# Routing the first expert layer in four parts of four tiles, and clearing the rows behind each expert with one indirect transfer

## The chip, the cores and the metric

The kernel runs on one core of one Trainium2 chip. The metric is the device time of one execution in microseconds (us). The profile is one execution recorded by the hardware profiler; its engines are PE (matrix multiply; PEld is its weight load), DVE (vector), ACT (scalar, activation functions), POOL (GpSimd, which also issues the indirect transfers) and SP (here a queue of transfers and register loads). Everything is float32.

## The reference

2048 tokens (8 sequences of 256) of width 128 pass six sub-layers, each added to the residual `x`:

```python
x = x + 0.5 * ffn0(layernorm(x))     # mixture of 8 experts, 2 of them per token
x = x + attention(layernorm(x))      # 16 heads of width 8
x = x + 0.5 * ffn0(layernorm(x))     # the same mixture and weights again
x = x + 0.5 * channel_mix(layernorm(x))
x = x + gated_conv(layernorm(x))
x = x + 0.5 * channel_mix(layernorm(x))
```

The change lies in the mixture, mostly in its first use:

```python
h = rmsnorm(x @ W_in.T, in_norm_w)
logits = h @ Wr.T
_, idx = top_k(logits + expert_bias, 2)
gates = softmax(logits[idx])         # zero for the experts that are not chosen
for e in range(8):
    oe = rmsnorm((silu(h @ Wg[e].T) * (h @ Wu[e].T)) @ Wd[e].T, enorm_w[e])
    out = out + gates[:, e:e+1] * oe
return rmsnorm(out, out_norm_w) @ W_out.T
```

## The kernel before

**Tiles and parts.** The tokens are 16 tiles of 128. `dispatch(f, i, parts, mp)` routes one part of the tiles for use `f` (0 or 1) of the mixture: `EARLY` lists the parts of the first use as (first tile, number of tiles), here (0, 2), (2, 2), (4, 4), (8, 4), (12, 4); `LATE` lists those of the second. A part is a list of nine or more stages: `turned` transposes x on PE and copies it out on ACT; `product` (two halves of up to two tiles) multiplies by the folded input weight, copies the result `u` and sums its squares on ACT; `measured` takes the layer norm's variance on DVE; `normed`, `logits` and `scaled` apply the norm; two `choice` stages find the two largest logits; `places` works out each token's row; `rows` scatters the tokens.

**Places.** Each expert owns a region of `REGION` = 2304 rows of the DRAM tensor `hss[f]`, and a token chosen by it takes the next free row. `prank` is that rank: a matmul with a triangle (earlier tokens of the tile, L418), one matmul with ones for each tile but the last of the part (earlier tiles of the part, L420), and one with `macc`, the counts of the earlier parts (L427). DVE then makes `at_row` (L437), the row numbers `pos`, and their integers `posi` (L445).

**Scatter.** `rows` issues two indirect transfers for each tile from POOL (L452), 128 rows of 516 bytes each: 32 for the whole use.

**Order.** `stagger(chunks, 4)` starts a part four stages after the one before it, so that two or three parts are interleaved. PE, DVE, ACT and SP run in the order in which the program issues, by hand; on POOL, what is marked with `keep_in_program_order` stays in order as well.

**Table, zeros, experts.** After the last part, `table` counts the rows of each expert (`pcnt`, L474) and works out on DVE which expert each of up to 24 row blocks belongs to and where it starts (`tab`; cast to integers by L528 and L531). For f = 0 it first calls `zeros(first)`, which writes 256 rows of zeros behind each expert's last row with eight transfers, four from SP and four from ACT; each one loads its row number into a register (L550) and writes 132 KB (L553). Then `experts` works through the blocks in the order `TURNS`: SP loads the expert number into a register and fetches the weights `w_f` (L593, 852 KB), loads the row number and fetches the rows `hst_f` (L599); PE turns them (`pht_f`, L605), DVE copies them (`ht_f`), PE multiplies by the gate and up weights (`pg_f`, `pu_f`, L615) and by the down weights (`py_f`, L638), and POOL scatters the results. A row fetch waits for all scatters and zeros of `hss[0]`. In the second use the zeros are written ahead of time by `clear_rows`, and rows are fetched ahead of weights.

**After it.** `attention` runs a written-out schedule of half steps in which the parts of the second dispatch are placed (`leaving`): the `places` of its three four-tile parts run inside the attention, the last two parts, of two tiles each, behind it.

Of the kernel before, what the change touches and what calls it, by code (L numbers as in the profile page):

```python
# [16 lines left out]
P = 128  # L17
# [30 lines left out]
EARLY = (0, 2), (2, 2), (4, 4), (8, 4), (12, 4)  # L48
# [16 lines left out]
def macaron_kernel(ctx: ExitStack, tc: tile.TileContext, a: dict, out: bass.AP):  # L65
# [44 lines left out]
    def pack(name, widths, rows=P):  # L110
# [10 lines left out]
    win, wr_t, inw, eb, tri, slot, base, order, tokid = pack(  # L121
        "pack1", [D, E, 1, E, P, 2, E, E, NCH * TPC * 2]
    )
    tokid = tokid.rearrange("p (t k) -> p t k", k=2).bitcast(I32)
# [4 lines left out]
    zero = const.tile([P, 2 * ROW], F32, tag="zero", name="zero")  # L129
    nc.vector.memset(zero, 0.0)  # L130
# [163 lines left out]
    nc.vector.tensor_reduce(wmean, win, AX.X, ALU.add)  # L294
    nc.vector.tensor_scalar(wmean, wmean, 1.0 / D, None, ALU.mult)
    nc.vector.tensor_scalar(win, win, wmean, None, ALU.subtract)
    wrn = const.tile([P, E], F32, tag="wrn", name="wrn")
    nc.vector.tensor_scalar(wrn, wr_t, inw, None, ALU.mult)
    pwr = bank("pwr", "sa")[:, 0 : D + E]
    nc.tensor.transpose(pwr[:, 0:D], win, ident)  # L300
    nc.tensor.matmul(pwr[:, D : D + E], win, wrn, start=True, stop=True)
    nc.scalar.copy(win_r, pwr)
# [17 lines left out]
    macc = const.tile([P, len(EARLY) + 1, E], F32, tag="macc", name="macc")  # L320
    nc.vector.memset(macc[:, 0, :], 0.0)

    def dispatch(f, i, parts, mp):
# [29 lines left out]
        def product(i):  # L353
# [9 lines left out]
            nc.scalar.copy(u, pp)  # L363
            sq = norm.tile([P, 2, D], F32, tag="sq", name=f"sqin_{n}_{i}")
            for j in range(2):
                t = 2 * i + j
                nc.scalar.activation(
                    sq[:, j], u[:, j, 0:D], AF.Square, accum_out=st["ss"][:, t : t + 1]
                )
# [43 lines left out]
        def places():  # L413
# [5 lines left out]
            for t in range(nt - 1):  # L419
                nc.tensor.matmul(  # L420
                    pr[:, t + 1 :, :],
                    ones,
                    mask[:, t : t + 1, :].to_broadcast([P, nt - 1 - t, E]),
                    start=False,
                    stop=False,
                )
            nc.tensor.matmul(  # L427
                pr, ones, macc[:, i : i + 1, :].to_broadcast(sh), start=False, stop=True
            )
            cnt = small.tile([P, E], F32, tag="cnt", name=f"cnt_{n}")  # L430
            nc.vector.tensor_reduce(cnt, mask.rearrange("p t e -> p e t"), AX.X, ALU.add)
            nc.vector.tensor_add(macc[:, i + 1, :], macc[:, i, :], cnt)
# [30 lines left out]
        if f == 0:  # L463
            return turned, *halves, measured, both(normed, logits, scaled), *choices, places, rows
        return turned, *halves, measured, normed, logits, scaled, *choices, places, rows

    def table(f, parts, mp):
# [5 lines left out]
        pc = bank(f"pcnt_{f}", "sb")[:, 0:E]  # L473
        nc.tensor.matmul(pc, ones, macc[:, len(parts), :], start=True, stop=True)  # L474
        cnt = t_([P, E], "cnt")
        nc.vector.tensor_copy(cnt, pc)
        if f == 0:
            first = t_([P, E], "first", I32)
            nc.vector.tensor_tensor(first, pc, base, ALU.add)
            zeros(first)  # L480
# [64 lines left out]

    def zeros(first):

        for e in range(E):
            queue = (nc.sync, nc.scalar)[e % 2]
            row = nc.values_load(  # L550
                first[0:1, e : e + 1], engines=[queue.engine], min_val=1, max_val=HS_ROWS - TT
            )
            ins = queue.dma_start(  # L553
                hss[0][bass.ds(row, TT), :].rearrange("(p r) w -> p (r w)", p=P), zero
            )
            tc.declare_no_dep(ins.ins, group="hs0", reason="rows of their own")
            tc.add_to_no_dep_group("hs0", ins.ins)
# [1026 lines left out]
```

## Time and profile before

| what | us |
|---|---|
| median of three runs (623.07 to 624.63) | 624.25 |
| the profiled execution's own time | 626.05 |
| its span, from the first to the last instruction | 624.1 |
| PE busy | 522.8 |
| DVE busy | 356.1 |
| ACT busy | 271.0 |
| POOL busy | 192.1 |
| first scatter of the first use starts on POOL | 16.67 |
| its last scatter starts | 63.57 |
| PE starts on the first expert block | 74.11 |

Positions in time are read from the start of the span. In a timeline line the first number is the start, the second how long the group took, then engine, line of the kernel, operation and tiles (written <- read); brackets hold the idle time of the engine before it and what ended it. "SPq" is the SP queue issuing a transfer. A waits line gives who waited for whom: total us, times, longest. The span is shorter than the execution's own time by what lies before the first and after the last instruction.

### The profile page before, as it was taken

How to read it: one execution, taken by the hardware profiler on the slowest of the kernel's cores; microseconds unless marked ns; L12 is line 12 of the kernel's file. 1: busy time of each engine (PE TensorE's matmuls, PEld its weight loads, DVE VectorE, ACT ScalarE, POOL GpSimd, SP SyncE). 2: the span in 40 equal slices, each digit the busy share in tenths (PEclk: the TensorE clock that was granted, in tenths of full speed). 3: DMA queues.
4: the chain of work that ended last, by engine and by line, in shares of the span. 5: the costliest groups of instructions: out<-in, count | busy, mean ns of one | idle time of the engine just before them, and what ended most of it. 6: DMA issues, size and time to landing. Idle time of an engine off the chain costs nothing.

```text
span 624.1 us, 11214 instructions
## 1 busy us (share of the span) xinstructions
PE 522.8 (84%) x3879; PEld 399.4 (64%) x3879; DVE 356.1 (57%) x1108; ACT 271.0 (43%) x662; POOL 192.1 (31%) x199
## 2 busy tenths in 40 slices
PE   4531299999989999899899987669999999889996
PEld 3521188898965555556556644449999984558884
DVE  3665255554443566767876884734444442777675
ACT  3532032222332455666765564213233232876265
POOL 0567135743343121001100446402333335520110
PEclk9999999999999999999999996599999998979999
DMA  6112647767723036408111001065778745000002
GB/s 224 35 38 94 202 154 211 207 194 219 218 79 102 27 43 174 168 35 257 51 49 22 26 26 51 31 217 178 216 222 252 216 137 147 1 0 2 2 1 67
DMA packets 38122, 71.70 MB, mean 115 GB/s; under 512 B 4587, under 2 KB 27922, under 8 KB 36912
## 3 DMA queue, kind: packets, MB, share of 16 engines
q1 hardware_dynamic: 33136, 61.97, 33.3%
q0 software_dynamic: 4352, 8.47, 3.9%
q8 instruction: 32, 0.52, 0.3%
q10 hardware_dynamic: 576, 0.53, 0.2%
q14 instruction: 26, 0.21, 0.1%
HBM read 50.10 MB, written 21.38 MB: 115 GB/s over the span
## 4 chain that ended last, share of the span: by engine, by line
PE 45%; ACT 9%; DVE 7%; DMA 5%; issue 3%; SPq 1%; POOL 0%; DVEq 0%; ACTq 0%; POOLq 0%
PE ps L967 8%; PE py_f L638 4%; PE pg_f L615 4%; PE pu_f L615 4%; ACT es L1004 4%; PE po L1014 4%; DMA y<-yrow_f,idx_f 3%; PE pvf L1343 2%; PE pgo L1370 2%; PE pm L950 1%; PE pk_m L1287 1%; DVE m L987 1%; PE pkv_m L1269 1%; PE pr_m L1269 1%; DMA w_f<-in_wall_dram 1%
## 5 line engine op out<-in xcount | busy, mean ns | idle before, releaser
L658 POOL DMA_INDIRECT y<-yrow_f,idx_f x72 | 70.7, 982 | 121.2 <-issue 61.8
L1004 ACT ACTIVATE es<-ps 128x1024 f32<-128x1024 f32 x64 | 65.3, 1020 | 51.7 <-PE ps L967 29.9
L987 DVE TENSOR_REDUCE m<-pm 128x4 f32<-128x1024 f32 x64 | 77.5, 1220 | 13.2 <-PE pm L950 13.1
L967 PE MATMUL ps<-qa,qk 32*128 32x256 f32 x512 | 72.8, 401 | 12.5 <-ACT es L1004 9.6
L452 POOL DMA_INDIRECT hs<-hrow,posi_f x64 | 61.7, 964 | 64.1 <-issue 28.7
L615 PE MATMUL pg_f<-ht_f,w_f 128*128 128x256 f32 (+1 forms) x336 | 71.5, 357 | 3.4 <-DMA w_f<-in_wall_dram 2.8
L638 PE MATMUL py_f<-w_f,hg_f 128*128 128x128 f32 x576 | 71.7, 276 | 2.4 <-issue 2.4
L950 PE MATMUL pm<-qk 32*128 32x256 f32 x512 | 73.1, 400 | 0.6 <-ACT qk L897 0.6
L638 PEld LDWEIGHTS py_f<-w_f,hg_f 128*128 128x128 f32 x576 | 69.5, 192 | 4.3 <-issue 2.7
L631 DVE TENSOR_TENSOR hg_f<-pu_f,sg_f 128x1024 f32<-128x1024 f32 (+1 forms) x42 | 45.0, 1071 | 43.4 <-PE pu_f L615 36.8
L615 PE MATMUL pu_f<-ht_f,w_f 128*128 128x256 f32 (+1 forms) x336 | 69.7, 350 | 0.0
L624 ACT ACTIVATE sg_f<-pg_f 128x1024 f32<-128x1024 f32 (+1 forms) x42 | 37.9, 901 | 59.5 <-PE pg_f L615 58.9
L967 PEld LDWEIGHTS ps<-qa,qk 32*128 32x128 f32 x512 | 43.6, 184 | 30.3 <-ACT es L1004 22.5
L648 ACT ACTIVATE ysq_f<-py_f 128x128 f32<-128x128 f32 x72 | 19.3, 273 | 99.6 <-PE py_f L638 92.1
L615 PEld LDWEIGHTS pg_f<-ht_f,w_f 128*128 128x128 f32 x336 | 56.1, 194 | 9.6 <-DVE hg_f L631 1.9
L615 PEld LDWEIGHTS pu_f<-ht_f,w_f 128*128 128x128 f32 x336 | 55.2, 192 | 5.6
L950 PEld LDWEIGHTS pm<-qk 32*128 32x128 f32 x512 | 44.2, 184 | 2.5 <-issue 1.5
L649 DVE TENSOR_TENSOR yrow_f<-py_f,w_f 128x256 f32<-128x256 f32 (+1 forms) x42 | 16.2, 387 | 45.0 <-ACT ysq_f L648 44.9
L607 DVE TENSOR_SCALAR ht_f<-pht_f,pack 128x256 f32<-128x256 f32 (+1 forms) x42 | 18.6, 444 | 33.5 <-PE pht_f L605 33.5
L605 PE MATMUL pht_f<-ident,hst_f 128*128 128x128 f32 x72 | 15.4, 283 | 24.5 <-DMA hst_f<-hs 24.5
L1014 PE MATMUL po<-es,v 128*32 128x256 f32 x512 | 35.7, 393 | 0.0
L161 POOL TENSOR_TENSOR cf_f<-cf_f,mhalf 128x8 f32<-128x8 f32 (+1 forms) x9 | 13.5, 1502 | 62.9 <-DVE cf_f L721 62.0
(271 smaller groups left out, 867.7 us busy)
## 6 DMA issues: line engine op xcount, KB each, us to landing
w_f<-in_wall_dram SPq DMA_DIRECT2D x41, 832.0 KB
hs<-blank SPq DMA_DIRECT2D x8, 1032.0 KB
hst_f<-hs SPq DMA_DIRECT2D x30, 129.0 KB
y_f<-y SPq DMA_DIRECT2D x14, 258.0 KB
pack<-in_pack_dram SPq DMA_DIRECT2D x1, 1729.0 KB
heads<-qkc SPq DMA_DIRECT2D x3, 512.0 KB
qk<-heads SPq DMA_DIRECT2D x12, 128.0 KB
y<-yrow_f,idx_f POOLq DMA_INDIRECT x72
```

Source lines behind the costliest of these rows:

```text
L452: ins = nc.gpsimd.indirect_dma_start(out=hss[f], out_offset=bass.IndirectOffsetOnAxis(ap=st["posi"][:, t, k : k + 1], axis=0), in_=hrow[:, ...
L615: nc.tensor.matmul(ph[:, k, :], w[t][:, o + k * P : o + k * P + P], ht[t], start=True, stop=True)
L624: nc.scalar.activation(sg, pg, AF.Silu)
L631: nc.vector.tensor_mul(hg[t], pu, sg)
L638: nc.tensor.matmul(py[:, s, :], hg[t][:, k, ts(s, P)], w[t][:, 2 * DFF + k * D : 2 * DFF + k * D + D], start=(k == 0), stop=(k == NFC - 1),)
L648: nc.scalar.activation(sq[:, s], py[:, s], AF.Square, accum_out=yrow[:, s, D : D + 1])
L658: ins = nc.gpsimd.indirect_dma_start(out=y2, out_offset=bass.IndirectOffsetOnAxis(ap=idx[:, s : s + 1], axis=0), in_=yrow[:, s, :], in_off ...
L950: nc.tensor.matmul(sc[:, jj, i, :], qs[c][r, g, col + i * P : col + (i + 1) * P], ks[c][r, g, col : col + S], start=True, stop=True,)
L967: nc.tensor.matmul(sc[:, jj, i, :], ks[c][r, g, col + i * P : col + (i + 1) * P], tops[s][r, :], start=True, stop=True,)
L987: nc.vector.tensor_reduce(m, sc, AX.X, ALU.max, negate=True)
L1004: nc.scalar.activation(es, sc, AF.Exp, scale=scale)
L1014: nc.tensor.matmul(po[32 * j : 32 * j + 32, :], vs[c][:, (b % 2) * 2 + i, (g % 2) * (H // 2) + (g // 2) * 4 + j, :], ess[s, j // 2][:, j % ...
```

## The change

- The first use is routed in four parts of four tiles, in place of five of which the first two had two tiles.
- In both uses the matmul for each tile of a part is dropped. DVE keeps a running count `ahead`, one entry for each tile, and one matmul with ones takes in the entries of the whole part.
- The first part's `u` is copied by DVE, while ACT squares straight out of PSUM; its `turned` and `measured` are issued in one stage.
- The input weight is folded inside a function `fold_in`, called after the attention's tiles are allocated; ahead of its matmuls PE multiplies the identity by itself nine times. DVE's norm statistics of the first part now come behind the folding.
- The eight zero transfers and their register loads are replaced by one indirect transfer from POOL: each of 128 partitions writes 16 rows (8256 bytes in a row) at a word offset that three small DVE operations work out. It stands behind the first scatter of the last part, with seven scatters behind it. Its source is part of an attention tile, set to zero by DVE at the start.
- `pcnt` is made ahead of the last part's `rows`.

```diff
-EARLY = (0, 2), (2, 2), (4, 4), (8, 4), (12, 4)
+EARLY = (0, 4), (4, 4), (8, 4), (12, 4)
...
-zero = const.tile([P, 2 * ROW], F32, tag="zero", name="zero")
-nc.vector.memset(zero, 0.0)
...
+    def fold_in():
...
+        warm_i = bank("warm_i", "sb")
+        for i in range(9):
+            nc.tensor.matmul(warm_i[:, ts(i % 4, P)], ident, ident, start=True, stop=True)
+        pwr = bank("pwr", "sa")[:, 0 : D + E]
+        nc.tensor.transpose(pwr[:, 0:D], win, ident)
+        nc.tensor.matmul(pwr[:, D : D + E], win, wrn, start=True, stop=True)
+        nc.scalar.copy(win_r, pwr)
...
-            nc.scalar.copy(u, pp)
+            first = f == 0 and t0 == 0
+            if first:
+                nc.vector.tensor_copy(u, pp)
+            else:
+                nc.scalar.copy(u, pp)
...
+                src = pp if first else u
                 nc.scalar.activation(
-                    sq[:, j], u[:, j, 0:D], AF.Square, accum_out=st["ss"][:, t : t + 1]
+                    sq[:, j], src[:, j, 0:D], AF.Square, accum_out=st["ss"][:, t : t + 1]
                 )
...
             nc.tensor.matmul(pr, tri, mask, start=True, stop=False)
-            for t in range(nt - 1):
-                nc.tensor.matmul(
-                    pr[:, t + 1 :, :],
-                    ones,
-                    mask[:, t : t + 1, :].to_broadcast([P, nt - 1 - t, E]),
-                    start=False,
-                    stop=False,
-                )
-            nc.tensor.matmul(
-                pr, ones, macc[:, i : i + 1, :].to_broadcast(sh), start=False, stop=True
-            )
-            cnt = small.tile([P, E], F32, tag="cnt", name=f"cnt_{n}")
-            nc.vector.tensor_reduce(cnt, mask.rearrange("p t e -> p e t"), AX.X, ALU.add)
-            nc.vector.tensor_add(macc[:, i + 1, :], macc[:, i, :], cnt)
+            for t in range(nt):
+                nc.vector.tensor_add(ahead[:, t0 + t + 1, :], ahead[:, t0 + t, :], mask[:, t, :])
+            nc.tensor.matmul(pr, ones, ahead[:, slots, :], start=False, stop=True)
...
+            start = both(normed, logits, scaled)
+            if i == 0:
+                return both(turned, measured), *halves, lambda: None, start, *choices, places, rows
+            return turned, *halves, measured, start, *choices, places, rows
...
+    def counts(f):
+        pc = bank(f"pcnt_{f}", "sb")[:, 0:E]
+        nc.tensor.matmul(pc, ones, ahead[:, NCH * TPC, :], start=True, stop=True)
+        return pc
+
+    def zeros(pc, mp):
+        at = mp.tile([P, E], F32, tag="zat", name="zat", bufs=1)
+        nc.vector.tensor_mul(at, pc, owner)
+        row = mp.tile([P, 1], F32, tag="zsum", name="zsum", bufs=1)
+        nc.vector.tensor_reduce(row, at, AX.X, ALU.add)
+        word = mp.tile([P, 1], I32, tag="zword", name="zword", bufs=1)
+        nc.vector.scalar_tensor_tensor(word, row, float(ROW), zrow, ALU.mult, ALU.add)
+        ins = nc.gpsimd.indirect_dma_start(
+            out=hss[0].rearrange("n w -> (n w)").unsqueeze(1),
+            out_offset=bass.IndirectOffsetOnAxis(ap=word, axis=0),
+            in_=blank[0],
+            in_offset=None,
+        )
...
-    def zeros(first):
-        for e in range(E):
-            queue = (nc.sync, nc.scalar)[e % 2]
-            row = nc.values_load(
-                first[0:1, e : e + 1], engines=[queue.engine], min_val=1, max_val=HS_ROWS - TT
-            )
-            ins = queue.dma_start(
-                hss[0][bass.ds(row, TT), :].rearrange("(p r) w -> p (r w)", p=P), zero
-            )
...
     def heads(hp):
         qks = [hp.tile([P, 2, 4, CT], F32, tag=f"qk{i}", name=f"qk{i}") for i in range(2)]
...
+        blank.append(qks[0].rearrange("p i g s -> p (i g s)")[:, 0 : 16 * ROW])
+        nc.vector.memset(blank[0], 0.0)
...
-            stagger([dispatch(0, i, EARLY, gp) for i in range(len(EARLY))], 4)
...
+                fold_in()
+                parts = [[*dispatch(0, i, EARLY, gp)] for i in range(len(EARLY))]
+                found = {}
+
+                def counted():
+                    found["pc"] = counts(0)
+                    zeros(found["pc"], gp)
+
+                parts[-1][-1] = both(counted, parts[-1][-1])
+                stagger(parts, 4)
...
+        "owner": p // 16 == e[None, :],
+        "zrow": ROW * (REGION * (p // 16) + 1 + 16 * (p % 16)),
```

## The prediction

> **What bounds the kernel now.** I read the page first, then who waited for whom in the first 80 us, then the timeline of that stretch, engine by engine.
>
> ```profile
> span 624.1 us, 11214 instructions
> ...
> PE   4531299999989999899899987669999999889996
> ...
> POOL 0567135743343121001100446402333335520110
> ```
>
> One slice is 15.6 us. From the sixth slice on PE is at 9 tenths nearly everywhere; ahead of that lie some 74 us in which PE does little. All the edits of weight lie there, so the question is what ends that stretch.
>
> ```profile
> PE pht_f L605 <- DMA hst_f<-hs: 21.8, 1, 21.8
> ```
>
> PE's longest wait by far is for the rows of the first expert block. Those need every scatter landed, the zeros landed, and SP free to issue the fetch. The timeline tells which was last:
>
> ```profile
> 16.67 1.17 POOL L452 DMA_INDIRECT hs<-hrow,posi_f  x1 [15.30 <-DVE z_f L351]
> ...
> 44.56 0.95 POOL L452 DMA_INDIRECT hs<-hrow,posi_f  x1 [1.77 <-issue]
> 45.82 0.95 POOL L452 DMA_INDIRECT hs<-hrow,posi_f  x1 [0.30 <-issue]
> ...
> 63.57 0.96 POOL L452 DMA_INDIRECT hs<-hrow,posi_f  x1 [0.30 <-issue]
> ```
> ```profile
> 55.09 12.76 SPq L553 DMA_DIRECT2D hs<-zero  x4
> 68.64 0.36 SPq L593 DMA_DIRECT2D w_f<-in_wall_dram  x1
> 69.86 0.41 SPq L599 DMA_DIRECT2D hst_f<-hs  x1
> ```
> ```profile
> 64.29 0.38 DVE L523 TENSOR_REDUCE tab_single<-tab_room 128x27 f32<-128x216 f32 x1 [3.12 <-issue]
> 66.39 0.18 DVE L528 CAST tab_tab<-tab_has 128x24 int32<-128x24 f32 x1 [0.50 <-DVE tab_has L524]
> 74.11 0.69 PE L605 MATMUL pht_f<-ident,hst_f 128*128 128x128 f32 x2 [21.82 <-DMA hst_f<-hs]
> ```
>
> Three chains end close together. POOL issues 32 scatters, one each 1.263 us (45.82 - 44.56) when it is fed; three times it isn't (gaps of 2.05, 4.58 and 1.77 us), and its last begins at 63.57. SP is held by four zero transfers until 67.85. DVE's table, begun at 52.4, has its first integers at 66.57: the same work without idle time is some 6 us, the rest is gaps of "issue". Then SP puts a weight load of 852 KB ahead of the row fetch, and the rows arrive 4.25 us after their issue (69.86 to 74.11). What this costs without SP's zeros is shown by the second use of the mixture, where the zeros are long written and rows are fetched ahead of weights:
>
> ```profile
> 404.83 0.96 POOL L452 DMA_INDIRECT hs<-hrow,posi_f  x1 [0.30 <-issue]
> 407.80 0.40 SPq L599 DMA_DIRECT2D hst_f<-hs  x1
> 410.17 0.42 PE L605 MATMUL pht_f<-ident,hst_f 128*128 128x128 f32 x2 [0.81 <-DMA hst_f<-hs]
> ```
>
> From the start of the last scatter to the fetch 2.97 us, to PE 5.34 us. Before the change the same distance is 10.54 us (63.57 to 74.11): 5.2 us are lost behind the scatters to SP and DVE, and 3 gaps of 8.4 us in all are lost ahead of them.
>
> **The change, part by part.**
>
> *When is the first part ready?* With two tiles its first scatter starts at 16.67. Four tiles add two transposes (0.21 each, by L337: four take 1.09, two 0.69) 0.4; a copy of 512 instead of 256 columns 0.2 (0.56 against 0.37); in product and squares 0.6 (two more matmuls take 0.9 and two more squares 0.6, but DVE now makes the copy of 0.39 beside ACT, and squares of half one run beside product two); eight or nine DVE steps on 32 instead of 16 columns 0.3. Then the rank's matmuls stand on PE behind the next part's product, which now has four matmul pairs (2.18 instead of 1.27), while one pair and 0.4 go: 0.5 to 0.8. Sum +2.0 to +2.3: 18.7 to 19.0. Against it stand the nine matmuls at the start. They need only the identity (ready at 1.37), are 18 passes at 0.21, 3.8 us, and end at 5.2, just where DVE has the folded weight ready (5.11), so they cost at most 0.3. Their worth is PE's clock:
>
> ```profile
> 75.43 3.75 PE L615 MATMUL pg_f<-ht_f,w_f 128*128 128x256 f32 x8 [0.62 <-issue]
> ...
> 81.38 1.89 PE L615 MATMUL pg_f<-ht_f,w_f 128*128 128x256 f32 x8
> ```
>
> The same eight matmuls take 3.75 us at the start and 1.89 after some 4 us of work. The Trainium skill ("TensorE: Matmul & The Clock Gate", Part 1) says the same of about 3.4 us of sustained work, and that one idle window of that length takes it back. By the first half the first part's transposes and products run at double pace (-1.3); by the second half PE's idle stretches of 3 to 4 us in the routing (4.16 ahead of the product at 27.12) make everything after that slow again. Trace alone (no warm start shown here): 18.9. Rule at its best, warm through part two: 16.7. I take warm for the first part only: 17.7.
>
> *Is POOL fed from then on?* A round of a four-tile part was 9.3 us (the `posi` of 22.7 to 32.06), of which DVE waited 2.41 for PE's rank:
>
> ```profile
> 27.12 2.18 PE L359 MATMUL pin_f<-win_r,xnt_f 128*128 128x136 f32 x8 [4.16 <-ACT xnt_f L339]
> ...
> 31.32 0.19 DVE L437 TENSOR_TENSOR at_row_f<-prank_f,pack 128x32 f32<-128x32 f32 x1 [2.41 <-PE prank_f L427]
> ```
>
> Three matmul pairs go (L420: 1.28); DVE loses a reduce and an add (0.38) and gains four adds in a row (0.2 each, from the 0.17 of macc's add and the step to the next), of which PE's second matmul needs three: 0.4 more DVE time, inside what is left of its wait. The round becomes 8.4. POOL needs 8 x 1.263 = 10.1 for a part, so it falls behind from the first part on and is never hungry; DVE gets 1.7 us of slack for each part. A stall such as the 4.66 us gap of DVE at 38 to 42.9 is covered from the second part on, and would cost up to 2 in the first.
>
> *POOL's chain.* 32 scatters and one zero transfer: the last starts 32 x 1.263 = 40.4 after the first, at 58.1. By the second use's distances the fetch follows at 61.1 and PE at 63.5: 10.6 earlier than 74.11.
>
> *The zeros.* No transfer of 8256 bytes from each partition is in the trace. On POOL's time: it has 128 rows and 128 offsets as a scatter has, so by the nearest row 0.96; if POOL paid for bytes, 16 rows' worth, 15.4. I take 0.96. On the DMA engines: 1.06 MB, issued at about 49; before the last scatter lands there are 7 x 1.263 + 2.5 = 11.3 us, 94 GB/s; the weights at 72 to 80 us ran at 357. Hidden. Its three DVE operations (0.5) are in slack. The rule against it: the skill's "SBUF — State Buffer" ("SBUF: two separate sides", the box on SWDGE and the part behind it) says that POOL can't write descriptors while DVE holds the port they share, and advises to issue from SP or ACT, the reverse of this edit. The trace disagrees for these shapes: at 44 to 64 DVE ran the choices and the table with two SBUF inputs, and POOL's pitch stayed 1.26 to 1.33. By the row the transfer costs 1.26; by the rule's 3.1 us for a blocked transfer, 2 us more.
>
> *Table and weights.* SP's zeros (12.8 us) and ACT's go whole. Part four's places end near 41; the table takes 14.2 us with the stalls of before, so SP can issue the first weights by 57 at the latest, without them by 49. They took 5.1 us to land (68.64 to 73.7), and the gate matmul needs them at 63.5 + 1.3. Covered by 2.9 us even with the stalls; beyond that each us of DVE is one of PE. The second weights are issued behind the first row fetch, as before, and PE needs them 7 us after its start, as before.
>
> *Second use.* For the three four-tile parts inside the attention PE waits for three adds behind DVE's `qa` (ended 339.47), where before the rank was done at 340.05: +0.35 each. In the last two parts one pair less, -0.43 each. Sum +0.2.
>
> *Other edits.* DVE's memset of 2064 columns (0.27 for 258; some 1.7 to 2.2) ends by 3.4, ahead of the pack, which DVE takes up at 4.27. The expert stage is unchanged and PE-bound, so the shift passes through.
>
> Sum: -10.6 + 0.2 = -10.4 on a span of 624.1, whose execution took 626.05, 1.8 over the median. I subtract from the median: 624.25 - 10.4 = 613.8.
>
> **Rivals.** *A. Part of it is taken back:* the first part comes late or POOL is hungry, the zero transfer costs 3 to 4, or the table's stalls grow past their cover of 2.9: 3 to 6 us lost, 617 to 620. For: DVE's gaps have no cause that the trace names. Against: POOL's queue grows by 1.7 a part.
> *B. Zeros priced by bytes on POOL:* the chain is then 14.4 longer, PE starts at 77.9, 3.8 later than before: 628. It decides from 11.6 us for that one instruction. Against: offsets, not bytes, are what it handles in every scatter seen.
> *C. The 74 us are not the bound:* if the expert stage had slack that took the shift, 624. Against: PE at 9 tenths, and `pg_f` L615 waits 3.4 us in 336 instructions.
>
> **Numbers.** Main forecast 0.75, A 0.15, B 0.05, C 0.03, and 0.02 for a gain under 0.3%. What a measurement of this kernel tells from no change is 0.3%, 1.9 us. The main range is 611 to 616 (first scatter at 16.7 to 18.9, second use -0.9 to +1); reaching into A gives 611 to 618. Faster 0.90 (main and A), same 0.05 (C and the small gain), slower 0.05 (B).
>
> **What would show it.** Right: the first scatter at 16.7 to 19; 33 POOL issues at a pitch of 1.26 without a gap over 0.5; the last near 58; the row fetch 3 us later with the first weights long issued; PE's first block near 63.5; the rest shifted by that. Wrong: a zero issue far over 1 us, gaps between POOL's parts, a weight load that lands after the rows, or an expert stage that grew.

## The result, and the profile after

The changed kernel takes 622.8 us (median of 22 runs, 618.9 to 630.3) where the kernel before takes 624.7 beside it: ratio 0.9962, interval 0.9944 to 0.998. The profiled execution took 623.28, its span is 621.5 against 624.1 before. So 2 to 3 us were gained where 10.4 were forecast, and the time lies above the range.

The page of the changed kernel, first by the slices of 15.6 us (busy tenths; PEclk is the clock that PE's throttle granted, in tenths of full speed):

```profile
span 621.5 us, 11085 instructions
...
PE   6411599999979999899899884669999998889996
...
POOL 0557146653333111101101345402343344520110
PEclk9655599999989999999999997599999998989999
```

PE's thin stretch still reaches into the fifth slice, and POOL has a slice with 1 tenth (the fifth: 62 to 78 us) behind one with 7: it was not through earlier. The timeline of the first 70 us shows the three chains that the prediction followed (start, duration, engine, line, tiles; in brackets the idle time before and who ended it):

```profile
6.44 1.12 PE L343 MATMUL pxt_f<-ident,x 128*128 128x128 f32 x4 [0.36 <-ACT win_r L306]
8.23 2.18 PE L365 MATMUL pin_f<-win_r,xnt_f 128*128 128x136 f32 x8 [0.68 <-ACT xnt_f L345]
19.23 1.17 POOL L453 DMA_INDIRECT hs<-hrow,posi_f  x1 [17.85 <-DVE amv_f L355]
...
38.38 0.95 POOL L453 DMA_INDIRECT hs<-hrow,posi_f  x1 [0.30 <-issue]
43.89 0.96 POOL L453 DMA_INDIRECT hs<-hrow,posi_f  x1 [4.55 <-issue]
...
55.25 0.96 POOL L485 DMA_INDIRECT hs<-qk,zword  x1 [0.30 <-issue]
...
64.30 0.96 POOL L453 DMA_INDIRECT hs<-hrow,posi_f  x1 [0.31 <-issue]
66.65 0.72 SPq L608 DMA_DIRECT2D hst_f<-hs  x1
68.81 0.69 PE L614 MATMUL pht_f<-ident,hst_f 128*128 128x128 f32 x2 [18.35 <-DMA hst_f<-hs]
```

POOL starts at 19.23, runs two parts without a gap, then waits 4.55 us for part two's places (counting from zero), and its last scatter begins at 64.30, later than before (63.57). The zero transfer costs POOL 0.96 us. The fetch follows the last scatter by 2.35 us, PE by 4.51: SP and the table are no longer in the way, and that is the whole gain at PE's first block, 74.11 to 68.81.

What did POOL wait for? DVE, ACT and PE in the same stretch:

```profile
29.48 0.19 DVE L417 TENSOR_REDUCE mx_f<-eq_f 128x4 f32<-128x32 f32 x1
...
32.84 0.19 DVE L415 TENSOR_TENSOR eq_f<-lb_f,mx_f 128x32 f32<-128x32 f32 x1 [1.23 <-DVE mx_f L413]
33.57 0.19 DVE L416 TENSOR_TENSOR eq_f<-eq_f,pack 128x32 f32<-128x32 f32 x1 [0.53 <-DVE eq_f L415]
34.27 0.19 DVE L417 TENSOR_REDUCE mx_f<-eq_f 128x4 f32<-128x32 f32 x1 [0.51 <-issue]
...
38.53 0.17 DVE L432 TENSOR_TENSOR ahead<-ahead,mask_f 128x8 f32<-128x8 f32 x1 [1.21 <-DVE ahead L432]
...
39.95 0.39 ACT L374 COPY u_f<-pin_f 128x272 f32<-128x272 f32 x1 [6.96 <-remote]
40.67 0.63 PE L433 MATMUL prank_f<-ahead,ones 128*128 128x32 f32 x2 [2.83 <-issue]
```

From 29.9 to 42.1 nearly each instruction starts 0.70 us, or twice that, after the one before it, on DVE, and ACT and PE stand as well, with nothing named that they wait for (`issue`, `remote`, their own last result). The instructions themselves take their usual 0.19. POOL alone goes on at its pitch as long as it has work. I call this a slow stretch. Code being loaded does not fill it: the profile counts one packet of instructions on the DMA queues from 28 to 44. Part two's places are done at 43.1 where a round of 8.4 us would have had them near 35. A second one lies on the table (55.5 to 65), hidden here by POOL. With this pattern known, the first trace has it too, at 56 to 67, where SP took 12.76 us for four zero issues, and in DVE's gap ahead of 42.88:

```profile
42.88 0.19 DVE L437 TENSOR_TENSOR at_row_f<-prank_f,pack 128x32 f32<-128x32 f32 x1 [4.66 <-remote]
```

PE's granted clock is low in the same slices of the changed kernel, but it is not the cause. From 20 to 72 us it is 0.51 here and 1.00 in the kernel before, which has slow stretches all the same, and one of the later profiles of the changed kernel (e14) has 0.52 from 12 to 68 and none.

### The profile page after: what moved, and what is told of

The parts are those of the page before. It is cut to its first block, busy times and chain, and to the rows that moved or that the text cites. A ratio compares the mean times of both kernels' runs of the same rounds, so it can differ in the third digit from the quotient of the medians.

```text
span 621.5 us, 11085 instructions
## 1 busy us (share of the span) xinstructions
PE 516.6 (83%) x3849; PEld 395.3 (64%) x3849; DVE 357.2 (57%) x1100; ACT 269.7 (43%) x658; POOL 193.2 (31%) x200
## 4 chain that ended last, share of the span: by engine, by line
PE 44%; ACT 10%; DVE 7%; DMA 5%; issue 2%; another core or an unknown queue 1%; SPq 1%; POOL 0%; DVEq 0%; ACTq 0%; POOLq 0%
PE ps L978 9%; PE py_f L647 4%; PE pg_f L624 4%; PE pu_f L624 4%; ACT es L1015 4%; PE po L1025 3%; DMA y<-yrow_f,idx_f 3%; PE pvf L1354 2%; PE pgo L1381 2%; DVE m L998 2%; PE pm L961 1%; PE pk_m L1298 1%; PE pr_m L1280 1%; PE pkv_m L1280 1%
## 5 line engine op out<-in xcount | busy, mean ns | idle before, releaser
L978 PEld LDWEIGHTS ps<-qa,qk 32*128 32x128 f32 x512 | 43.7, 184 | 30.3 <-ACT es L1015 21.8
```

The lines of the kernel that those rows point to most:

```text
L978: nc.tensor.matmul(sc[:, jj, i, :], ks[c][r, g, col + i * P : col + (i + 1) * P], tops[s][r, :], start=True, stop=True,)
```

## The experiments

Three chips did these runs: chip A (e1 to e4, e9 to e11; the kernel before takes 623.5 to 624.4 there), chip B (e5 to e8; 615.8) and chip C (e12 to e18; 615.5, and 620.9 in the last session). Ratios are to the kernel before on the same chip in the same session. Traces differ as much between chips as between kernels, so each reading below names its chip. Theory 1: a long train of scatters on POOL (one behind the other without a gap) slows the other engines. Theory 2: the stall belongs to a place in the instruction stream. Theory 3: only the late first part costs. The first pair of traces looks like chip A's. Theory 4 came after e5 to e8: the chip's condition decides whether there is a slow stretch at all.

**e1, every scatter of the first use twice** (chip A)

```
-                for k in range(2):
+                for k, to in ((0, hss[f]), (1, hss[f]), (0, spare), (1, spare))[: 2 if f else 4]:
...
-                        out=hss[f],
+                        out=to,
```

> Every scatter of the first use is issued a second time, into a DRAM tensor of its own that nobody reads; all else is the changed kernel. Theory 1 (an unbroken train of indirect transfers on POOL makes DVE, ACT, PE and SP step at about 0.70 us an instruction, from some 8 to 12 us after the train's first transfer until some 3 us after its last): a part now has 16 transfers, 20.2 us, more than a slow round, so the train is unbroken from 19.2 to about 99, and the slow stretch lasts from about 29 to about 102; DVE's steps in parts two, three and four and in the table are all 0.7 apart; PE's first block is at 106 or later. Theory 2 (the stall belongs to a place in the instruction stream[...]): DVE is slow in part two's places (29.9 to 42.1) and again in the table, and at full pace in part three, as in the changed kernel. Theory 3 (only the late first part costs; the slow stretches are chance): no stretch of 0.70 us steps need be there, parts come at 8.4 us.

POOL ran 48 transfers from 17.63 without a gap:

```profile
77.17 0.96 POOL L454 DMA_INDIRECT spare<-hrow,posi_f  x1 [0.30 <-issue]
86.18 0.95 POOL L486 DMA_INDIRECT hs<-qk,zword  x1 [8.05 <-DVE tab_cnt L503]
```
```profile
57.02 0.19 DVE L398 TENSOR_TENSOR lg_f<-u_f,ri_f 128x32 f32<-128x32 f32 x1 [2.38 <-remote]
58.42 0.19 DVE L410 TENSOR_TENSOR lb_f<-lg_f,pack 128x32 f32<-128x32 f32 x1 [1.21 <-DVE lg_f L398]
...
85.03 0.22 DVE L442 TENSOR_REDUCE pos_f<-both_f 128x8 f32<-128x64 f32 x1 [0.48 <-DVE both_f L440]
85.28 0.17 DVE L447 CAST posi_f<-pos_f 128x8 int32<-128x8 f32 x1
```

DVE's slow steps began near 29 and lasted to 85: the whole of part three, which ran at full pace in the changed kernel, now crept. When the train ran dry they stopped, some 8 us after its last transfer began (3 were expected). Theory 2 falls. Theory 1's detail was off in one point: slow parts took longer than the 20 us that POOL needs for one, so the train did break once, at 78. PE's first block came at 108.8, and the one execution took 667.2. The profile counts one packet of instructions from 28 to 86.

**e2, a memset of 192 columns on POOL behind every scatter of the first use** (chip A, one profile)

```
+                    if f == 0:
+                        tc.keep_in_program_order(nc.gpsimd.memset(pause, 0.0))
```

> A small memset on POOL after every scatter of the first use, so that the pitch becomes some 1.5 to 1.8 instead of 1.263 us. Theory 1, if it is the rate that fills something up: no slow stretch, parts two to four ready at the 8.4 us round (posi at about 18.9, 27.3, 35.7, 44.1), table without steps of 0.70; the last scatter 32 pitches after 19.2, at 67 to 77, and PE's first block 5.3 after it. Theory 1, if it is the unbroken train and not its rate: the slow stretch comes as in the changed kernel. Theory 2: slow at part two's places (29.9 to 42.1) all the same.

```profile
20.95 0.96 POOL L455 DMA_INDIRECT hs<-hrow,posi_f  x1 [0.17 <-issue]
21.91 0.27 POOL L465 MEMSET pause<- 128x192 f32 x1
22.35 0.97 POOL L455 DMA_INDIRECT hs<-hrow,posi_f  x1 [0.17 <-issue]
...
34.50 0.33 DVE L448 CAST posi_f<-pos_f 128x8 int32<-128x8 f32 x1
...
64.23 0.96 POOL L455 DMA_INDIRECT hs<-hrow,posi_f  x1 [0.17 <-issue]
68.71 0.69 PE L618 MATMUL pht_f<-ident,hst_f 128*128 128x128 f32 x2 [26.38 <-DMA hst_f<-hs]
```

At a pitch of 1.40 us POOL is never hungry, the parts' places come each 7.7 to 8.2 us (26.27, 34.50, 42.22), and apart from three steps at 43 to 45.4 the slow stretch is gone. It gained nothing: the pauses cost 32 x 0.137 = 4.4 us of POOL, as much as the hunger had, and PE starts at 68.71.

**e3, the old counting in the second use** and **e4, no warming matmuls** (chip A)

```
+            if f == 0:
...
+            else:
+                for t in range(nt - 1):
+                    nc.tensor.matmul(
+                        pr[:, t + 1 :, :],
...
+                    pr, ones, macc[:, i : i + 1, :].to_broadcast(sh), start=False, stop=True
...
+                nc.vector.tensor_reduce(cnt, mask.rearrange("p t e -> p e t"), AX.X, ALU.add)
+                nc.vector.tensor_add(macc[:, i + 1, :], macc[:, i, :], cnt)
```

```
-        warm_i = bank("warm_i", "sb")
-        for i in range(9):
-            nc.tensor.matmul(warm_i[:, ts(i % 4, P)], ident, ident, start=True, stop=True)
```

> The second use of the mixture counts as in the kernel before (matmul pairs and a running sum by part), the first use as in the changed kernel. Theory 1: the earlier rank joined two groups of scatters into one train of eight at 372 to 382; with the old rank the gaps of 0.85 and 0.95 us come back, the slow stretch is the 3 us of before instead of 8, and the 3.3 us that were lost between 375 and 420 return: profile span about 618, ratio to the kernel before about 0.991 (the changed kernel has 0.996). Rival (what is lost at 375 to 420 comes from the shift itself, not from the counts): span 621.5, ratio 0.996.

> The nine warming matmuls on the identity are left out; nothing of the result depends on them. If they do nothing for PE's clock in the first part (as the changed kernel's 2.18 us for eight product matmuls at 8.23 suggests): pwr at about 5.1, first scatter at 18.9 to 19.3, ratio to the kernel before 0.996 as with them. If they warm it for part of the way: first scatter 0.3 to 1.3 later, PE's first block and the end later by the same, ratio 0.997 to 0.998.

e3 gave 0.9889 (0.9833 to 0.9945, six runs), its profile a span of 619.2. That is near the number of theory 1, but its trace does not bear the reason: one gap of 2.48 us did come back into the train, and yet DVE stood still between 373 and 381 again,

```profile
376.57 0.16 DVE L387 SCALAR_TENSOR_TENSOR ri_f<-ss_f,z_f 128x2 f32<-128x2 f32 x1 [3.45 <-ACT u_f L376]
380.75 0.17 DVE L392 RECIPROCAL ri_f<-ri_f 128x2 f32<-128x2 f32 x1 [4.03 <-ACT warm L133]
```

and the way from the attention's last maximum to the second experts' first product took 51.3 us, against 49.7 in the changed kernel. Most of this standing still is PE and not a slow stretch. PE's granted clock is 0.50 from 368 to 380, and the four product matmuls there take 1.28 us, where the changed kernel's first profile has 1.00 and 0.73. The changed kernel on chip C (e18), with 0.50 from 364 to 372, has nearly the same waits:

```profile
372.36 0.16 DVE L385 SCALAR_TENSOR_TENSOR ri_f<-ss_f,z_f 128x2 f32<-128x2 f32 x1 [3.46 <-ACT sqin_f L379]
375.35 0.17 DVE L390 RECIPROCAL ri_f<-ri_f 128x2 f32<-128x2 f32 x1 [2.83 <-ACT ri_f L389]
```

That leaves 1.2 us of e3's two waits for a slow stretch. e4 and e11, with the new counts, have e3's waits too (3.46 and 4.03, 3.45 and 4.14), so they are not what the old counts brought. e3's six times lie in two groups, 615.3 to 616.5 and 621.1 to 622.6, and the profile is of the second. What its span gained on the changed kernel's first profile lies at the front. There its nine matmuls did find PE at its fast pace:

```profile
6.44 0.66 PE L345 MATMUL pxt_f<-ident,x 128*128 128x128 f32 x4 [0.36 <-ACT win_r L306]
7.77 1.19 PE L367 MATMUL pin_f<-win_r,xnt_f 128*128 128x136 f32 x8 [0.68 <-ACT xnt_f L347]
```

Half the time of the same rows above (1.12 and 2.18), and its first scatter is at 17.83 instead of 19.23. Of the 16 profiles with these nine matmuls 13 have a warm first part (the product's matmuls at the fast pace), with the first scatter at 17.3 to 17.8 (15.7 in e8, whose first part has two tiles); three are cold (19.2 to 19.3), the changed kernel's first profile among them. Without the matmuls (e4) the first part was cold, first scatter 18.91, ratio 0.9957 (0.9929 to 0.9984). The worth of the warming, 1.3 us where it works, is below what the timed runs tell apart.

**e5, e6, e7, e8** (chip B): memsets of 8 columns (e5) and of 192 (e6) behind every scatter of both uses; the old zeros in the changed kernel (e7); the old five parts in it (e8)

```
+PAUSE = 8
...
+                    tc.keep_in_program_order(nc.gpsimd.memset(pause, 0.0))
```

```
-                    zeros(found["pc"], gp)
...
+            nc.vector.tensor_tensor(first, pc, base, ALU.add)
+            old_zeros(first)
```

```
-EARLY = (0, 4), (4, 4), (8, 4), (12, 4)
+EARLY = (0, 2), (2, 2), (4, 4), (8, 4), (12, 4)
```

(`PAUSE` is 192 in e6; `old_zeros` is the function `zeros` of the kernel before.)

> A memset of 8 columns on POOL after every scatter of both uses, so that the pitch grows by less than with 192 columns (1.40 us instead of 1.263, which ended the slow stretch of parts two to four). Theory 1a (the rate of the transfers fills something, which drains at 1.40): at a pitch under 1.30 the slow stretch comes as in the changed kernel or one to three us later, POOL is hungry for some 4 us again, PE's first block stays near 68 to 69, ratio to the kernel before 0.994 to 0.998. Theory 1b (any other POOL instruction between two transfers breaks the train, whatever the rate): no slow stretch in either use, last scatter at 19.2 (or 17.7 with a warm first part) + 32 x 1.28 = 60.2 (58.7), PE's first block 4.5 to 5.3 later, second use 6 us shorter; ratio 0.98.

> The memset of 192 columns after every scatter, now in both uses. Theory 1: the second use has no stretch of 0.70 us steps at 375 to 385 either; PE's wait of 6.64 us for ACT's copy of osb, and DVE's of 8.14, go; at most 0.14 x 4 are added by the slower pitch behind the last places. PE starts the first use's blocks at 68.7 as with pacing there alone; the second use's blocks start 6 to 8 us earlier than in the changed kernel: span 614 to 616, ratio to the kernel before 0.984 to 0.987. Rival (the wait at 375 to 385 is another thing than that in the first use, as its engines then also run the attention): span 621, ratio 0.996.

> The zeros as in the kernel before (eight transfers at register addresses on SP's and ACT's queues, behind the table's counts), all else as in the changed kernel. By the prediction's step on the zeros: SP is held by its four for 12.8 us behind the first counts (tab_cnt at about 52), with a slow stretch on top, so the row fetch comes at 69 to 70 and PE's first block at 73 to 74, some 5 later than in the changed kernel; POOL has one issue less, its last scatter at about 63. Rival (the zeros were hidden anyway behind POOL's last scatter): row fetch at 66 to 67 and PE at 68 to 69.

> The first layer in the five parts of before (2, 2, 4, 4, 4 tiles), with the changed kernel's counts, zeros and warming. Theory 1: trains of four from about 16, with gaps, so the first slow stretch comes later than 29.9 (in the kernel before at 38.2), but POOL is hungry between the two-tile parts; last scatter at 61 to 64, PE's first block 4.5 to 5.3 later, ratio to the kernel before 0.993 to 0.998: as good as four parts. Rival (four-tile parts are what saves the time, as the prediction had it): last scatter over 64, ratio 0.999 or more.

None of the four has a slow stretch, with or without pauses: e8 ran 24 scatters at full pace from 30.3 and DVE kept its steps of 0.22. So e5 and e6 could not tell 1a from 1b here, and theory 4 was needed. The rest is still of use. e5: 0.9926 (0.9901 to 0.9952), PE's first block at 64.5. e6: 0.9993 (0.9971 to 1.0014), where 0.984 to 0.987 was expected: where nothing crawls, pacing only costs. e8: 1.0006 (0.9985 to 1.0027), last scatter at 60.68 and PE at 65.14, with gaps of 1.62 and 3.29 us left between the short parts' scatters. So without the four parts nothing was gained, where 0.993 to 0.998 was expected. The gaps are not all of it: e5, on the same chip, is at PE only 0.6 us earlier, and its median is 4.8 lower. e7, of which I had expected 5 us of loss:

```profile
41.62 4.08 SPq L579 DMA_DIRECT2D hs<-qk  x4
...
59.41 0.42 SPq L625 DMA_DIRECT2D hst_f<-hs  x1
```

SP's four zero issues take 4.08 us, not 12.76, and are over nearly 14 us ahead of the fetch. PE starts at 61.66, the earliest of all runs: without a slow stretch the zeros were hidden on SP, and moving them onto POOL's chain costs its place there (1.26 us; against e14, on another chip, PE is 1.1 earlier).

**e9, e10, e11** (chip A again): the kernel before, the changed kernel, and e5's kernel

> The kernel before, unchanged, for its trace on the chip on which the next two run. If the slow stretches of 0.70 us steps belong to a long train of transfers on any chip (theory 1), they are at 38 to 43 and 56 to 67 as in the first trace, and PE's first block is at 74. If a chip must also be in a certain condition (theory 4: in the last four runs, on a chip on which the kernel before takes 615.8, unbroken trains of 16 and more showed no slow stretch), there are none on such a chip: table done by 57 or earlier, last scatter near 60, SP's zeros the last of the three chains, PE's first block at 66 to 69.

> The changed kernel, unchanged, on the same chip. Theory 1: slow stretch from some 10 us into each train, PE's first block at 68 to 69, ratio 0.996. Theory 4 on a chip without slow stretches: POOL is fed without a gap, 33 issues at 1.263, the last at 58.1 to 59.7 (first scatter 17.7 with a warm first part, 19.2 without), row fetch 2.3 to 3.0 later, PE's first block 4.5 to 5.3 later, at 62.6 to 65; the kernel before has its first block at 66 to 69 there, so 3 to 5 us are gained, ratio 0.992 to 0.995.

> The changed kernel with a memset of 8 columns on POOL after every scatter of both uses, again. On a chip with slow stretches: theory 1a (rate) has them as in the changed kernel, since the pitch is 1.273 instead of 1.263; theory 1b (any POOL instruction between the transfers breaks the train) has none, last scatter at 58.5 to 60 and ratio 0.98 to 0.985. On a chip without them: as the changed kernel, to within 1 us.

Slow stretches in all three. e9 repeats the first trace (PE at 74.61). e10: warm start, first scatter 17.34, hunger of 4 us at 36.5 to 41.8, last scatter 62.08, PE at 66.66; ratio 0.9962 (0.9947 to 0.9978). e11: the same hunger at a pitch of 1.27 (36.81 to 42.14), PE at 67.81, ratio 0.9981 (0.9957 to 1.0005). So a POOL instruction between the scatters is not enough (1b falls); with e2's single profile the pitch is what matters on this chip (1a): 1.27 crawls, 1.40 does not.

**e12 and e16, trains by themselves in the attention** (chip C): 12 paced full rows, 14 short rows, 22 full rows at full pace, into DRAM that nobody reads

```
+                at(4, "b", partial(train, 12, 1000 + ROW, 0, True))
+                at(11, "b", partial(train, 14, 16, 1, False))
+                at(19, "b", partial(train, 22, ROW, 2, False))
```

> The changed kernel with three trains of extra transfers in the attention, where POOL is otherwise idle, into DRAM that nobody reads: 12 full rows of 516 bytes with a memset of 152 columns behind each (pitch 1.36 to 1.38) at 223 to 240; 14 short rows of 64 bytes at the full pace at 262 to 281; 22 full rows at the full pace at 304 to 333. Each adds one small copy on DVE; the rest is unchanged. On a chip whose first use shows a slow stretch: theory 1 by the bytes or writes: only the third train has one, from 8 to 12 us after its start (314) to 3 us after its end, costing the attention 10 us or more; by the number of transfers or descriptors: the second has one too, in its last 6 to 10 us; by the routing's own work and not the train (rival): none of the three has one. The paced train should have none. On a chip without slow stretches: none anywhere, whole kernel within 2 us of the changed kernel.

> The kernel with the three extra trains in the attention, unchanged, in case this chip has slow stretches in the first use. By the bytes or writes: only the third train (22 full rows at full pace) has one, from 8 to 12 us after its start, costing the attention 10 us or more. By the number of transfers: the second (14 short rows) has one too in its last 6 to 10 us. By the routing's own work and not the train: none. On a chip without slow stretches: the third train costs the attention under 1 us, as on the chip before.

No slow stretch anywhere, so bytes and number could not be told apart. What it does show: on such a chip the 22 full rows cost the attention 0.7 us (e12) and 1.4 us (e16), measured as the extra delay of its maxima against e14 (under 1 was expected). The first use is e14's to 0.2 us.

**e13, e14, e15, e17, e18** (chip C): e6's kernel; the changed kernel; the kernel before; pauses of 192 columns in the second use's four-tile parts alone; the changed kernel beside that

```
+                    if paced:
+                        tc.keep_in_program_order(nc.gpsimd.memset(pause, 0.0))
```

> The changed kernel with the memset of 192 columns behind every scatter of both uses, again, beside the changed kernel on the same chip. On a chip with slow stretches: first use as with pacing there alone (last scatter 62.7 to 64.2, PE's first block 67.2 to 68.7, the same as the changed kernel's), second use without the wait of 8 us of DVE: 5 to 6 us faster than the changed kernel; ratio to the kernel before 0.986 to 0.990. On a chip without them: 4 us slower than the changed kernel by the pitch (32 x 0.137), ratio 0.996 to 1.000.

> The changed kernel, unchanged, on the same chip. With slow stretches: PE's first block at 66.7 to 68.8, ratio 0.996. Without them (theory 4): 33 POOL issues without a gap, last at 58.1 to 59.7, PE's first block at 62.6 to 65; ratio 0.990 to 0.995.

> The kernel before, unchanged, for its trace on the same chip. With slow stretches: as in the first trace, PE's first block at 74 to 75. Without them: last scatter near 60, no stretch of 0.70 us steps at 38 to 43 or 56 to 67, PE's first block at 66 to 69.

> The changed kernel with the memset of 192 columns behind the 24 scatters of the second use's three four-tile parts alone; first use and the last eight scatters unchanged. On a chip with slow stretches: first use as the changed kernel (PE's first block at 66.7 to 68.8), the second without DVE's wait of 8 us: 3 to 6 us under the changed kernel, ratio to the kernel before 0.986 to 0.991. On a chip without them: within 1 us of the changed kernel, ratio 0.994 to 0.997.

> The changed kernel, unchanged, on the same chip, to stand beside the paced one: with slow stretches PE's first block at 66.7 to 68.8, without them at 62.6 to 65; ratio 0.994 to 0.997 in either case.

e15 and e14 are the pair on which the forecast can be tried without a slow stretch. The kernel before:

```profile
32.90 0.96 POOL L452 DMA_INDIRECT hs<-hrow,posi_f  x1 [4.56 <-issue]
...
51.34 3.83 SPq L553 DMA_DIRECT2D hs<-zero  x4
...
62.09 0.96 POOL L452 DMA_INDIRECT hs<-hrow,posi_f  x1 [0.30 <-issue]
64.38 0.41 SPq L599 DMA_DIRECT2D hst_f<-hs  x1
66.54 0.69 PE L605 MATMUL pht_f<-ident,hst_f 128*128 128x128 f32 x2 [16.61 <-DMA hst_f<-hs]
```

The changed kernel:

```profile
17.63 1.17 POOL L453 DMA_INDIRECT hs<-hrow,posi_f  x1 [16.25 <-DVE amv_f L355]
...
49.48 0.96 POOL L485 DMA_INDIRECT hs<-qk,zword  x1 [0.30 <-DVE tab_tab L565]
...
58.32 0.96 POOL L453 DMA_INDIRECT hs<-hrow,posi_f  x1 [0.30 <-issue]
60.62 0.40 SPq L608 DMA_DIRECT2D hst_f<-hs  x1
62.77 0.69 PE L614 MATMUL pht_f<-ident,hst_f 128*128 128x128 f32 x2 [22.68 <-DMA hst_f<-hs]
```

After goes by the forecast's own figures (17.7, 58.1, 61.1 and 63.5 were written). But the kernel before, without its slow stretches, is at PE by 66.54 instead of 74.11. The difference is 3.8 us; e14's ratio is 0.9946 (0.9925 to 0.9968). e13 lost the pitch, 0.9998 (0.9973 to 1.0023). e17 has 0.9898 (0.9857 to 0.9938) and e18 0.9863 (0.9832 to 0.9894), with the kernel before at 620.9 this time: no gain from pacing the second use where nothing crawls. Both lie under the 0.994 to 0.997 that was expected; the changed kernel's own median is 612.6 here and 612.1 in e14, so it was the kernel before that was slower. Why the kernel before took 5 us longer in that session than in the one before it on the same chip, no trace of it tells.

No version stood clearly ahead of the changed kernel on its own chip. e3 comes nearest (its interval ends at 0.9945, e10's begins at 0.9947), on six runs, in another session, and with a trace that does not say why. On chip B the changed kernel itself was not run.

## Why the prediction was wrong, step by step

Starts of the same events in three pairs of profiles, us (the last maximum of the attention is DVE's last `m`; products are DVE's `hg_f`):

| | PE's first block | last maximum | second experts' first product | their second product | span |
|---|---|---|---|---|---|
| first pair, before | 74.11 | 370.52 | 417.88 | 423.36 | 624.1 |
| first pair, after | 68.81 | 366.54 | 416.22 | 422.13 | 621.5 |
| chip A, e9 before | 74.61 | 370.43 | 418.55 | 422.89 | 623.7 |
| chip A, e10 after | 66.66 | 364.32 | 415.04 | 423.41 | 624.4 |
| chip C, e15 before | 66.54 | 362.81 | 408.42 | 412.19 | 613.1 |
| chip C, e14 after | 62.77 | 358.85 | 402.55 | 410.58 | 610.1 |

- **The step that failed: "it falls behind from the first part on and is never hungry", and with it "a stall such as the 4.66 us gap of DVE at 38 to 42.9 is covered from the second part on".** The gap was taken for a piece of bad luck of fixed size. It was a slow stretch, which comes with long trains of scatters on such a chip; the forecast put the cost of a full queue to the other engines at nothing. Feeding POOL without gaps makes the train longer: the stretch grew from 4.7 to 12.2 us and began at 29.9, in part two's places. POOL stood 4.55 us, 4.25 more than its usual 0.30.
- **The sum of the first pair.** Forecast to measured at PE's first block is 63.5 to 68.81, +5.3: first scatter +1.5 (19.23 against 17.7), hunger +4.25, a pitch above 1.263 in the first and some late transfers +0.4, distance from the last scatter to PE -0.8 (4.51 against 5.34). In the span of this pair, 5.3 us were gained at PE's first block, 1.3 of them lost up to the attention's last maximum and 2.8 up to the second experts' second product, and 1.4 gained behind it: 2.6.
- **Where the expected 10.6 came from, the second step that failed.** The reading "5.2 us are lost behind the scatters to SP and DVE" was true of that trace and wrong as a cost of the code: SP's 12.76 us for four issues and the table's stalls were a slow stretch as well. Without it the four take 3.83 and the last scatter bounds: from its start to PE are 4.45 us in e15, and 4.45 in e14 too, so of the 5.2 nothing was there to gain. So 7.6 us of the 74.11 (less 66.54) were no cost of the code. Of the 8.4 us of gaps ahead of the last scatter 0.9 are POOL's usual 0.30 and 1.5 the slow stretch ahead of 42.88. What is left on chip C is POOL's two gaps behind the short parts, 1.74 and 4.26 us above the usual 0.30, less 1.26 for the zero transfer and 1.05 for a later first scatter: 3.7, and 3.8 was measured.
- **First scatter.** The forecast's bounds were 16.7 and 19.0, its value 17.7. Measured: 17.3 to 17.8 warm, 18.9 to 19.3 cold. The value was right for 13 of the 16 profiles and not for the first; which of the two comes differs from execution to execution, and the forecast had one value for both.
- **The zeros.** 0.96 us on POOL was right, and rival B is out. That DMA hides it was right: the row fetch follows the last scatter by 2.3 us with it (e14) and without it (e7). That it also frees SP was right only where SP crawls; otherwise e7 shows the move as a loss of 1.1 us at PE (61.66 on chip B against e14's 62.77 on chip C, one profile each).
- **The shared port.** The worry of the Trainium skill's rule ("SBUF — State Buffer", "SBUF: two separate sides"), that POOL would be held up by DVE, showed in no run beyond 0.12 us: POOL's pitch was 1.26 to 1.27 for most of the time that all other engines crawled, and 1.38 at the most. It was the others that paid.
- **Second use and the pass-through.** +0.2 was forecast. From the last maximum to the second product the kernel before takes 52.8, 52.5 and 49.4 us in the three pairs, the changed one 55.6, 59.1 and 51.7: 2.3 to 6.6 were lost again there. In the first pair and e10 (whose profiled execution, at 626.1 us, is the longest of its 22) it is mostly a slow stretch that now lies on the last parts:

```profile
377.19 0.16 DVE L385 SCALAR_TENSOR_TENSOR ri_f<-ss_f,z_f 128x2 f32<-128x2 f32 x1 [2.00 <-ACT u_f L374]
385.49 0.17 DVE L390 RECIPROCAL ri_f<-ri_f 128x2 f32<-128x2 f32 x1 [8.14 <-ACT ri_f L389]
```

  where before DVE waited 3.05, and 2.19 in e14 and e15. In e14 PE waits for the expert weights and then works at a slower pace, with a granted clock of 0.79 from 404 to 412:

```profile
404.88 2.38 PE L624 MATMUL pg_f<-ht_f,w_f 128*128 128x256 f32 x8 [2.44 <-DMA w_f<-in_wall_dram]
407.48 2.98 PE L624 MATMUL pu_f<-ht_f,w_f 128*128 128x256 f32 x8
```

  These two take 1.97 and 1.89 in both profiles of the first pair. From the start of the first to the second product are 5.70 us instead of 4.02, so the pace is 1.7 of the 2.3; in e10 it is 5.71, so 1.7 of the 6.6 as well. "The expert stage is unchanged, so the shift passes through" held up to the last maximum on chip C (3.8 us gained at the first block, 4.0 there). In the first pair and on chip A 1.3 and 1.8 were lost by then, and no run says to what.
- **Rival A** had the mechanism in its words ("POOL is hungry, or the table's stalls grow", "DVE's gaps have no cause that the trace names"). It got 0.15 and 3 to 6 us, since the queue's slack of 1.7 us a part was set against it. On a chip with slow stretches it is what happened at the first block, and the second use took back 2.8 more, so that 622.8 lies above its 617 to 620 as well.

Not settled: what fills up. The runs say that on chip A it begins five to ten transfers into a train at 1.27 us or faster, that it ends 3 to 8 us after the train's last begins, that a slower pace ended it (one profile), and that chips B and C do not have it at trains of 22 to 33. Whether it goes by bytes or by number could not be tried where it would have shown. Nor is it settled why e3 was faster.

## What to carry to other kernels

A gap for which the trace names no cause, and which several engines have at the same time on the same grid of steps, is not idle time that a reordering gets to use: ask what else ran, and whether the change makes more of that. Do not count such a gap both as a cost of the code that happened to stand in it and as removed with that code. And when one queue is to be kept full, price what its fullness does to the others, and look at the same pair on a second chip before a gain of some per mille is believed.

## What the runs showed of the hardware

- During unbroken trains of indirect transfers (128 rows of 516 bytes, pitch 1.263) DVE, ACT, PE and SP start most instructions only each 0.70 us or a multiple, from five to ten transfers into the train until 3 to 8 us after its last begins; POOL keeps its pitch, to 0.12 us. On chip A in the first use of every profile without the pause of 192 columns, on B and C in none.
- A memset of 192 columns between the transfers (0.27 us, pitch 1.40) ended it on chip A, one of 8 columns (pitch 1.27) did not.
- The same kernel took 624 us on chip A and 615.5 to 615.8 on B and C (620.9 on C in another session); of the 11 us between the spans of the first and of e15, 7.6 are gone by PE's first block.
- Four us of matmuls from 1.43 on gave the first products (at 7.2 to 8.3 us) the fast pace in 13 of 16 profiles (1.19 us for eight matmuls), and not in three (2.18).
- PE's granted clock can fall to 0.50 for tens of us (20 to 72 in the changed kernel's first profile). In the routing, where PE mostly waits, that showed no cost: the first expert block's first eight matmuls take 3.75 us there and in the kernel before, whose clock was 1.00. So the row alone does not give the pace, as these matmuls take 1.89 at 1.00 six us later. In the second use the same matmuls took up to 1.8 times as long (1.28 us against 0.73).
